# The next image's Walsh transform is moved beside its norms, its convolution is let in one pair at a time, and GpSimd gets no transform

## The chip, the cores and the metric

The kernel runs on one core of a Trainium2 chip. The metric is device time in microseconds (us). Before the change it is 11163.44 us, the median of three runs (11158.33 to 11166.24); the profiled execution has a span of 11170.1 us. Times inside the program are given as us from the start of that span. PE is TensorE, DVE VectorE, ACT ScalarE, POOL GpSimd, and SP issues most of the transfers. All numbers are 32-bit floats.

## The reference, cut to what matters

Four layers follow one another. The first two hold the Mamba scans and take the span up to about 9080 us; the change doesn't touch them. The last stage of the kernel holds the layers 2 and 3, for four images of 192 channels and 64 x 64 points:

```python
# layer 2: depthwise 3x3 convolution; its weights come from a small network on the pooled image.
# MASK keeps the upper row and the left neighbour: four taps a channel
wt = wt.reshape(b * DIM, 1, K, K) * jnp.tile(MASK, (b, 1, 1, 1))
out = jax.lax.conv_general_dilated(x.reshape(1, b * c, h, w), wt, ...)
...
# layer 3
xn = layer_norm(x.transpose(0, 2, 3, 1), norm1_g, norm1_b).transpose(0, 3, 1, 2)
xw = get_window(xn)                  # 4x4 windows: 16 positions, each of 192 channels
wf = sedenion_full_weight(w_sed)     # wf[i, k] = sum_j SED_TABLE[i, j, k] * w_sed[j]
xw = xw @ wf
x1 = reverse_window(xw, c)
y = x1.transpose(0, 2, 3, 1)
y = jax.nn.gelu(y, approximate=False)
y = y @ proj_w + proj_b
x = x + y.transpose(0, 3, 1, 2)
hbr = layer_norm(x.transpose(0, 2, 3, 1), norm2_g, norm2_b)
hbr = jax.nn.gelu(hbr @ fc1_w + fc1_b, approximate=False)
hbr = hbr @ fc2_w + fc2_b
x = x + hbr.transpose(0, 3, 1, 2)
```

In the sedenion product, output position k takes input i with weight i XOR k, with a sign. With signs put on inputs, weights and outputs, most of the 256 terms become a plain XOR convolution. A Walsh transform over the 16 positions turns that into 16 separate products. The terms whose sign does not fit are added directly from the normed input.

## The kernel before

The 16 positions are kept as 8 pairs g (the code's `NP`), each a tile of 128 partitions x 3 x 256. One image b goes through: convolution of 8 pairs (`prepare`), norm of each pair (`first_norm`), Walsh transform (`forward`), 16 products (`spectrum`), transform back (`inverse`), then for each pair k the direct terms (`product`), projection and second norm (`project`), and the two-layer network (`mlp`).

`Lanes` is a static scheduler. The main program emits matmuls and calls `tick()` between small groups of them; each tick lets each lane emit one more piece. So it fixes the order of the instructions on every engine. At run time each engine takes its own in that order and waits with semaphores.

```python
xh = const.tile([128, NP + 2, 3, NWIN], F32, name="xh")   # 10 slots for transformed pairs
at = list(range(NP))                                       # slot of each pair
spare = deque(range(NP, NP + 2))                           # two free slots

def normed(v, which, sq):                 # used by both norms
    mean = bank("mean"); each(full(mean), ones, v, [ALL, ALL])          # PE
    d = work.tile([128, 3, NWIN], F32, name=f"d{which}", bufs=1)
    nc.vector.tensor_tensor(d[:, 0::2, :], v[:, 0::2, :], mean[:, :, W], ALU.subtract)
    ...                                                                 # two more for the middle part
    nc.scalar.activation(sq, d, AF.Square)
    yield 3
    var = bank("var"); each(full(var), ones, sq, [ALL, ALL])            # PE
    nc.scalar.activation(rs, var[:, :, W], AF.Sqrt, bias=eps)
    nc.vector.reciprocal(rs, rs)
    nc.gpsimd.tensor_tensor(d[:, 0::2, :], d[:, 0::2, :], rs, ALU.mult) # and two more on GpSimd
    ...
    yield 6
    return d

def prepare(b):                           # convolution, lane 2
    for g in range(NP):
        i2, j = divmod(g, WIN)
        if j == 0:
            img = first if b == i2 == 0 else load(b, i2)   # 8 transfers, one buffer
        while g >= XW and (b, g - XW) not in read:
            yield 1
        v = work.tile([128, 3, NWIN], F32, name="xw", bufs=XW)
        for c in range(3):
            for tap in (3, 0, 1, 2):
                ...  # tap 3 on ACT (affine), taps 0 to 2 on DVE (scalar_tensor_tensor)
                yield 1
        nc.sync.dma_start(kept[b, g], v)
        lanes.add(3, first_norm(b, g, v))

def first_norm(b, g, v):                  # lane 3
    d = yield from normed(v, 1, sq)
    ...                                   # three affine on ACT: xn (image 0) or sq
    if b:
        nc.sync.dma_start(stored[b, g], t)    # put by in DRAM until the image's turn
    ready.add((b, g))

def butterfly(engine, s, d, a, b):
    engine.tensor_tensor(s, a, b, ALU.add)
    engine.tensor_tensor(d, a, b, ALU.subtract)

def both(v, to):                          # the transform's step inside a pair
    ...                                   # ACT: two copies into swapped
    butterfly(nc.vector, to[:, 0, :], to[:, 2, :], v[:, 0, :], v[:, 2, :])
    nc.vector.scalar_tensor_tensor(to[:, 1, :], v[:, 1, :], flip, swapped, ALU.mult, ALU.add)

def across():                             # the three steps across pairs: 12 butterflies
    n = 0
    for bit in (4, 2, 1):
        for a in range(NP):
            if a & bit:
                continue
            s, d = at[a], at[a | bit]
            to = spare.popleft()
            engine = nc.gpsimd if n % 3 == 1 else nc.vector
            butterfly(engine, xh[:, to], xh[:, d], xh[:, s], xh[:, d])
            at[a] = to; spare.append(s); n += 1
            yield 1

def forward(b):                           # lane 4
    for g in range(NP):
        both(xn[b, g], xh[:, at[g]]); yield 1
    yield from across()
    turned.add(b)

def inverse(b):                           # lane 4
    yield from across()
    for g in range(NP):
        ...  # both(xh[:, old], xh[:, to]) through a spare slot
        back.add((b, g)); yield 1

def product(b, k):
    for cols, made in zip((main, side), slots(k)):
        ps = psum_s.tile([128, 2, 2, NWIN], F32, name="sed_ps")   # two such tiles in all
        ...                               # PE: 92 records a pair in the profile; a tick between slots
        lanes.until(lambda: (b, k) in back)
        ...                               # DVE: six additions of ps and xh into y

lanes.add(4, walsh_weights())             # 24 GpSimd instructions, into xh as scratch
lanes.add(2, prepare(0))
for b in range(NB):
    lanes.until(lambda: (b, NP - 1) in ready and "weights" in turned)
    if b:
        fetch(b)                          # 8 loads of xn from DRAM
    lanes.add(4, forward(b))
    lanes.until(lambda: b in turned)
    if b + 1 < NB:
        lanes.add(2, prepare(b + 1))
    for g in range(NP):
        spectrum(g)
    lanes.add(4, inverse(b))
    for k in range(NP):
        ...
        lanes.add(0, project(b, k, product(b, k), x3))
lanes.drain()
```

Of the kernel before, what the change touches and what calls it, by code (L numbers as in the profile page):

```python
# [21 lines left out]
NB = 4  # L22
# [1057 lines left out]
def conv_and_windows(tc, x, sums, packs, aps, out):  # L1080
# [11 lines left out]
    with ExitStack() as ctx:  # L1092
# [100 lines left out]


        xh = const.tile([128, NP + 2, 3, NWIN], F32, name="xh")
        at = list(range(NP))
        spare = deque(range(NP, NP + 2))
        w_main = const.tile([128, 16, C], F32, name="w_main")
        w_side = const.tile([128, NP, C], F32, name="w_side")

# [36 lines left out]
            return d  # L1237

        xn, kept, stored, outs = {}, {}, {}, {}
        read, ready, projected, through, closed = set(), set(), set(), set(), set()  # L1240
        turned, back = set(), set()

        def prepare(b):

            for g in range(NP):
                i2, j = divmod(g, WIN)
                if j == 0:
                    img = first if b == i2 == 0 else load(b, i2)
                while g >= XW and (b, g - XW) not in read:
                    yield 1  # L1250
                v = work.tile([128, 3, NWIN], F32, name="xw", bufs=XW)
                for c in range(3):
                    for tap in (3, 0, 1, 2):
                        o = v[:, c, :].rearrange("p (r c) -> p r c", c=HW // WIN)
                        at = j + tap % 3
                        src = img[:, c, :, tap // 3, at : at + HW - 3 : WIN]
                        wk = wt[:, c, tap, b : b + 1]
                        if tap == 3:
                            affine(o, src, wk, w["bias"][:, c : c + 1])
                        else:  # L1260
                            nc.vector.scalar_tensor_tensor(o, src, wk, o, ALU.mult, ALU.add)  # L1261
                        yield 1
                kept[b, g] = dram.tile([128, 3, NWIN], F32, name="kept", bufs=2 * NP)
                nc.sync.dma_start(kept[b, g], v)
                lanes.add(3, first_norm(b, g, v))

        def first_norm(b, g, v):

            sq = work.tile([128, 3, NWIN], F32, name="sq", bufs=1)
            d = yield from normed(v, 1, sq)  # L1270
            read.add((b, g))
            if b == 0:
                t = xn[b, g] = work.tile([128, 3, NWIN], F32, name="xn", bufs=NP)
            else:
                t = sq
            n = norm1[x_sign[position(g, 0)], x_sign[position(g, 1)]]
            for c in range(3):
                affine(t[:, c, :], d[:, c, :], n[:, 0, c : c + 1], n[:, 1, c : c + 1])
            if b:
                stored[b, g] = dram.tile([128, 3, NWIN], F32, name="ahead", bufs=NP)  # L1280
                nc.sync.dma_start(stored[b, g], t)
            ready.add((b, g))

        def fetch(b):
            for g in range(NP):
# [3 lines left out]
        def butterfly(engine, s, d, a, b):  # L1289
            engine.tensor_tensor(s, a, b, ALU.add)  # L1290
            engine.tensor_tensor(d, a, b, ALU.subtract)  # L1291

        def walsh_weights():


            for j in range(16):
                if w_sign[j] > 0:
                    nc.scalar.activation(sed[:, :, j, :], sed[:, :, j, :], AF.Copy, scale=-1.0)

            def split(v, bit):  # L1300
                return v.rearrange("p (h e l) -> p e h l", e=2, l=bit * C)

            one, two = (xh[:, 4 * i : 4 * i + 4].rearrange("p a b c -> p (a b c)") for i in range(2))
# [12 lines left out]

        def both(v, to):

            swapped = work.tile([128, NWIN], F32, name="swapped", bufs=2)
            for k in range(2):  # L1320
                nc.scalar.copy(swapped[half[k], :], v[half[1 - k], 1, :])
            butterfly(nc.vector, to[:, 0, :], to[:, 2, :], v[:, 0, :], v[:, 2, :])
            nc.vector.scalar_tensor_tensor(  # L1323
                to[:, 1, :], v[:, 1, :], flip, swapped, ALU.mult, ALU.add
            )

        def across():

            n = 0
            for bit in (4, 2, 1):  # L1330
                for a in range(NP):
                    if a & bit:
                        continue
                    s, d = at[a], at[a | bit]
                    to = spare.popleft()
                    engine = nc.gpsimd if n % 3 == 1 else nc.vector
                    butterfly(engine, xh[:, to], xh[:, d], xh[:, s], xh[:, d])
                    at[a] = to
                    spare.append(s)
                    n += 1  # L1340
                    yield 1

        def forward(b):
            for g in range(NP):
                both(xn[b, g], xh[:, at[g]])
                yield 1
            yield from across()
            turned.add(b)

        def inverse(b):  # L1350
            yield from across()
            for g in range(NP):
                to, old = spare.popleft(), at[g]
                both(xh[:, old], xh[:, to])
                at[g] = to
                spare.append(old)
                back.add((b, g))
                yield 1
# [7 lines left out]

        main, side = slice(0, 128), slice(128, C)

        def spectrum(g):

            v = xh[:, at[g]]
            ps, ends, sides = parts()
            for outs, cols in ((ends, main), (sides, side)):
                for start in (True, False):
                    for k in range(2):
                        if start:
                            wt, x = w_main[:, position(g, k), cols], v[:, 2 * k, :]
                        else:
                            wt, x = w_side[half[k], g, cols], v[half[k], 1, :]
                        nc.tensor.matmul(outs[k], wt, x, start=start, stop=not start)  # L1380
# [3 lines left out]
            nc.scalar.activation(v[:, 0::2, :], ps[:, :, W], AF.Copy, scale=-1.0 / 32)  # L1384

        def slots(k):

# [13 lines left out]
        def product(b, k):  # L1401


            y = work.tile([128, 3, NWIN], F32, name="y", bufs=2)
            for cols, made in zip((main, side), slots(k)):
# [5 lines left out]
                left = Counter(group(t) for slot in made for t in slot)  # L1411
                begun = set()
                for slot in made:
# [18 lines left out]
                v = xh[:, at[k]]  # L1432
                if cols == side:
                    nc.vector.tensor_tensor(y[:, 1, :], ps[:, 1, 0, :], v[:, 1, :], ALU.add)
                    nc.vector.tensor_tensor(y[:, 1, :], ps[:, 0, 0, :], y[:, 1, :], ALU.add)
                else:
                    for h in (1, 0):
                        for s in range(2):
                            o = y[:, 2 * s, :]
                            nc.vector.tensor_tensor(o, ps[:, h, s, :], o if h == 0 else v[:, 2 * s, :], ALU.add)  # L1440
            return y

        def signed_gelu(k, y):
# [80 lines left out]
        lanes.add(4, walsh_weights())  # L1524
        lanes.add(2, prepare(0))
        for b in range(NB):
            lanes.until(lambda: (b, NP - 1) in ready and "weights" in turned)
            if b:
                fetch(b)
            lanes.add(4, forward(b))  # L1530
            lanes.until(lambda: b in turned)
            if b + 1 < NB:
                lanes.add(2, prepare(b + 1))
            for g in range(NP):
                spectrum(g)
# [161 lines left out]
```

## Time and profile before

| in the whole span of 11170.1 us | busy us | share |
|---|---|---|
| PE (matmuls) | 9265.0 | 83% |
| DVE | 9136.7 | 82% |
| ACT | 6545.5 | 59% |
| POOL | 7206.1 | 65% |

The last stage begins with the first load of an image at 9082.7 us. The table below gives its parts by what PE executes; the borders are those used for the windows of the profile.

| stretch, us | length | PE busy | DVE busy | what it is |
|---|---|---|---|---|
| 9753 to 10233 | 480.0 | 383.73 | 248.90 | image 1, from the end of image 0's last product |
| 10120 to 10194 | 74.0 | 72.61 | 20.35 | two pairs late in image 1 |
| 10760 to 10800 | 40.0 | 37.78 | 9.46 | image 3, the products of the spectrum |
| 10800 to 10840 | 40.0 | 24.31 | 30.57 | image 3, the transform back |

How to read it: a share of busy time over the whole span says little here, since four fifths of it belong to the scans. A stage has to be read from windows, from who waits for whom in it, and from the instructions in order of time. In the window view each engine's busy time is followed by its number of instructions, and the last three columns are the TensorE clock that was granted (1.00 is full), the share of the DMA engines and GB/s. A matmul instruction of this program appears as two records.

### The profile page before, as it was taken

How to read it: one execution, taken by the hardware profiler on the slowest of the kernel's cores; microseconds unless marked ns; L12 is line 12 of the kernel's file. 1: busy time of each engine (PE TensorE's matmuls, PEld its weight loads, DVE VectorE, ACT ScalarE, POOL GpSimd, SP SyncE). 2: the span in 40 equal slices, each digit the busy share in tenths (PEclk: the TensorE clock that was granted, in tenths of full speed). 3: DMA queues.
4: the chain of work that ended last, by engine and by line, in shares of the span. 5: the costliest groups of instructions: out<-in, count | busy, mean ns of one | idle time of the engine just before them, and what ended most of it. 6: DMA issues, size and time to landing. Idle time of an engine off the chain costs nothing. (4 is left out here: it accounts for less than half of the span.)

```text
span 11170.1 us, 97554 instructions
## 1 busy us (share of the span) xinstructions
PE 9265.0 (83%) x31324; PEld 3673.1 (33%) x31324; DVE 9136.7 (82%) x7831; ACT 6545.5 (59%) x9766; POOL 7206.1 (65%) x2768
## 2 busy tenths in 40 slices
PE   7888888888878888887689999999999854978788
PEld 2222222222223222222233333333333322545455
DVE  7999999999999999999688888788878837364542
ACT  5666666666666666666466666666666613333333
POOL 6888888888888888888466566566656622021110
PEclk7777777777777777777789889898889866989899
DMA  5666666666666666666455454454445422122110
GB/s 149 178 178 179 182 172 181 180 173 183 175 182 178 175 179 176 182 179 171 123 138 141 128 140 133 128 137 135 133 129 137 125 47 54 36 51 46 37 30 19
DMA packets 954743, 1506.97 MB, mean 135 GB/s; under 512 B 229834, under 2 KB 262638, under 8 KB 953846
## 3 DMA queue, kind: packets, MB, share of 16 engines
q1 hardware_dynamic: 953006, 1493.27, 49.8%
q10 hardware_dynamic: 1224, 7.47, 0.2%
q8 instruction: 247, 4.05, 0.2%
q14 instruction: 266, 2.18, 0.1%
HBM read 1289.65 MB, written 210.76 MB: 134 GB/s over the span
## 5 line engine op out<-in xcount | busy, mean ns | idle before, releaser
L570 DVE TENSOR_TENSOR_SCAN h<-dA,m_state,h 128x512 f32<-128x512 f32 x3840 | 4670.9, 1266 | 487.7 <-ACT dA L564 425.3
L586 POOL TENSOR_TENSOR h<-h,C 128x2048 f32<-128x2048 f32 x960 | 4342.0, 4527 | 625.8 <-ACT m_state L583 520.4
L564 ACT ACTIVATE dA<-dtE,m_A 128x512 f32<-128x512 f32 x4608 | 3106.1, 687 | 1308.8 <-DVE h L570 1194.2
L557 DVE TENSOR_TENSOR h<-dtxE,B 128x2048 f32<-128x2048 f32 x960 | 2170.6, 2261 | 116.8 <-DMA dtxE<-r_dtx 104.1
L595 PE MATMUL y<-h,gather 128*32 128x512 f32 x7680 | 1283.0, 747 | 402.3 <-POOL h L586 329.1
L448 PE MATMUL ps_in<-xT,m_in_w 96*128 96x512 f32 x1536 | 948.6, 765 | 250.4 <-ACT raw L451 132.0
L1233 POOL TENSOR_TENSOR d<-d,rs 128x512 f32<-128x512 f32 x64 | 86.5, 1351 | 1419.1 <-DVE rs L1232 1419.1
L466 PE MATMUL ps_conv<-raw,m_conv 128*128 128x512 f32 x2112 | 992.7, 619 | 1.7 <-ACT xc L471 1.7
L570 DVE TENSOR_TENSOR_SCAN h_apart<-dA,m_state,h_apart 128x512 f32<-128x512 f32 x768 | 922.5, 1260 | 39.6 <-ACT dA L564 39.6
L586 POOL TENSOR_TENSOR h_apart<-h_apart,C 128x2048 f32<-128x2048 f32 x192 | 869.4, 4528 | 45.6 <-ACT m_state L583 43.4
L557 POOL TENSOR_TENSOR h_apart<-dtxE,Bs 128x2048 f32<-128x2048 f32 x192 | 869.5, 4529 | 6.0 <-ACT Bs L546 6.0
L448 PEld LDWEIGHTS ps_in<-xT,m_in_w 96*128 96x128 f32 x1536 | 352.2, 242 | 821.9 <-issue 422.5
L585 POOL COPY m_state<-h 128x4 f32<-128x4 f32 x384 | 71.9, 187 | 850.0 <-DVE h L570 815.3
L466 PEld LDWEIGHTS ps_conv<-raw,m_conv 128*128 128x128 f32 x2112 | 418.2, 202 | 602.2 <-issue 568.1
L992 PE MATMUL ps_dw<-strip,dw 96*96 96x512 f32 x1152 | 574.4, 646 | 1.3 <-ACT x L1001 0.9
L595 PEld LDWEIGHTS y<-h,gather 128*32 128x32 f32 x7680 | 164.2, 117 | 1213.8 <-POOL h L586 570.2
L502 POOL TENSOR_TENSOR raw<-dt,xc 128x1536 f32<-128x1536 f32 x96 | 329.8, 3436 | 293.8 <-ACT dt L501 293.8
L482 PE MATMUL ps_x<-xc,m_pack 128*44 128x512 f32 x576 | 351.0, 758 | 198.0 <-ACT xc L478 194.7
L1421 PE MATMUL sed_ps<-xn,sed 64*128 64x256 f32 (+3 forms) x2944 | 496.1, 413 | 15.7 <-DVE y L1440 15.7
L564 ACT ACT_TABLE_LOAD x345 | 442.6, 1283 | 14.8 <-DMA dtE<-r_dt 8.5
L448 PE MATMUL ps_in<-xn,m_in_w 96*128 96x512 f32 x768 | 398.7, 666 | 47.4 <-ACT z L451 31.1
L375 PE MATMUL ps_o<-hid,t 128*96 128x512 f32 x768 | 390.8, 649 | 37.2 <-ACT hid L368 16.9
(192 smaller groups left out, 12506.9 us busy)
## 6 DMA issues: line engine op xcount, KB each, us to landing
dtE<-r_dt SPq DMA_DIRECT2D x2304, 256.0 KB, 5.0
dtxE<-r_dtx SPq DMA_DIRECT2D x2304, 256.0 KB, 4.2
r_dt<-dt SPq DMA_DIRECT2D x96, 768.0 KB, 4.0
r_dtx<-raw SPq DMA_DIRECT2D x96, 768.0 KB, 6.0
x<-x SPq DMA_DIRECT2D x64, 384.0 KB, 3.6
img<-x SPq DMA_DIRECT2D x28, 512.0 KB, 7.1
xt<-in_x SPq DMA_DIRECT2D x32, 384.0 KB, 5.6
x<-o SPq DMA_DIRECT2D x32, 384.0 KB, 4.9
```

Of the source, the lines that this page charges most:

```text
L375: nc.tensor.matmul(ps, self.w2[:, m, bass.ts(k, CP)], h[:, m, :], start=(m == 0), stop=(m == NH - 1),)
L448: nc.tensor.matmul(ps, self.in_w[:, k, bass.ts(e, 128)], xn[:, k, :], start=(k == 0), stop=(k == 1))
L466: nc.tensor.matmul(ps, self.conv[:, d, j, :], raw[:, d, j : j + T], start=(j == 0), stop=(j == K - 1))
L482: nc.tensor.matmul(ps, self.x_w[:, d, :], xc[:, d, :], start=(d == 0), stop=(d == ND - 1))
L502: nc.gpsimd.tensor_tensor(dtx, dt, xc, ALU.mult)
L557: engine.tensor_tensor(h, u["rows", k // 2, 1], u[B, k % 2].unsqueeze(1).broadcast_to([128, 4, T]), ALU.mult)
L564: self.nc.scalar.activation(dA, u["rows", k // 2, 0][:, j, :], AF.Exp, scale=self.A[:, k, j : j + 1])
L570: self.nc.vector.tensor_tensor_scan(h[:, j, :], u.pop(("dA", k, j)), h[:, j, :], self.state[:, k, j : j + 1], ALU.mult, ALU.add,)
L586: nc.gpsimd.tensor_tensor(h, h, u["C", k % 2].unsqueeze(1).broadcast_to([128, 4, T]), ALU.mult)
L595: self.nc.tensor.matmul(u["ys"][32 * j : 32 * j + 32, :], self.ex.gather[:, i // 2, :], h[:, j, :], start=(i == 0), stop=(i == 3 and not s ...
L992: nc.tensor.matmul(ps, dw[:, k, j, :], s[:, k, dy : dy + rows, dx : dx + HW], start=(j == 0), stop=(j == 8),)
L1421: nc.tensor.matmul(out, sed[p, int(h is not None), i ^ position(k, s), cols], xn[b, g][p, c, :], start=group(t) not in begun, stop=left[gr ...
```

## The change

The transform of an image no longer waits for all its norms and for its turn. Each norm of the next image goes on to `both` into a slot of `xh`, and then takes all butterflies for which the pairs are there (`settle`). Slots come free one at a time, as `product(k)` of the image in work has read its own. The transform back is also done step by step as the spectrum's products come in. The next image's convolution of pair g is let in only when the image in work has reached pair g - 1, and its pieces are spaced by two ticks. All butterflies are on DVE. The scratch of `walsh_weights` moves from `xh` to two work tiles whose names are used later. In image 0, where nothing else runs, the norms alternate between two lanes with a `d` each.

```diff
-        at = list(range(NP))
-        spare = deque(range(NP, NP + 2))
+        at = [[None] * NP for _ in range(NB)]
+        spare = deque(range(NP + 2))
...
 def prepare(b):
-                while g >= XW and (b, g - XW) not in read:
+                while g >= XW and (b, g - XW) not in read or b and g > reached[b - 1] + 1:
                     yield 1
...
-                        yield 1
+                        yield 2 if b else 1
...
-                lanes.add(3, first_norm(b, g, v))
+                lanes.add(1 if b == 0 and g % 2 else 3, first_norm(b, g, v))
 def first_norm(b, g, v):
-            sq = work.tile([128, 3, NWIN], F32, name="sq", bufs=1)
-            d = yield from normed(v, 1, sq)
+            i = 2 if b == 0 and g % 2 else 1
+            sq = work.tile([128, 3, NWIN], F32, name="sq", tag=("sq", "xn2")[i - 1], bufs=i)
+            if b:
+                yield 3
+            d = yield from normed(v, i, sq)
...
-            ready.add((b, g))
+            while settled[b] < g or len(spare) < 2:
+                yield 1
+            at[b][g] = spare.popleft()
+            both(t, xh[:, at[b][g]])
+            yield 1
+            yield from settle(at[b], g)
+            settled[b] += 1
...
-        def across():
-            ... engine = nc.gpsimd if n % 3 == 1 else nc.vector
+        def settle(v, g):
+            for bit in (1, 2, 4):
+                if (g + 1) % (2 * bit):
+                    return
+                for a in range(g + 1 - 2 * bit, g + 1 - bit):
+                    s, d, to = v[a], v[a + bit], spare.popleft()
+                    nc.vector.tensor_tensor(xh[:, to], xh[:, s], xh[:, d], ALU.add)
+                    nc.vector.tensor_tensor(xh[:, d], xh[:, s], xh[:, d], ALU.subtract)
+                    v[a] = to
+                    spare.append(s)
                     yield 1
-        def forward(b): ...
         def inverse(b):
-            yield from across()
+            for g in range(NP):
+                while (b, g) not in made:
+                    yield 1
+                yield from settle(at[b], g)
...
 def product(b, k):
+            spare.append(at[b][k])
             return y
...
         for b in range(NB):
-            lanes.until(lambda: (b, NP - 1) in ready and "weights" in turned)
+            lanes.until(lambda: settled[b] == NP and "weights" in turned)
             if b:
                 fetch(b)
-            lanes.add(4, forward(b))
-            lanes.until(lambda: b in turned)
             if b + 1 < NB:
                 lanes.add(2, prepare(b + 1))
+            lanes.add(4, inverse(b))
             for g in range(NP):
-                spectrum(g)
-            lanes.add(4, inverse(b))
+                spectrum(b, g)
             for k in range(NP):
                 n = b * NP + k
+                reached[b] = k
```

More of the change, by code (lines that the diff above doesn't have):

```diff
@@ L1239, in conv_and_windows @@
         xn, kept, stored, outs = {}, {}, {}, {}
-        read, ready, projected, through, closed = set(), set(), set(), set(), set()
-        turned, back = set(), set()
+        read, projected, through, closed = set(), set(), set(), set()
+        turned, made, back = set(), set(), set()
+        settled = [0] * NB
+        reached = [-1] * NB
         def prepare(b):
@@ L1287, in fetch @@
                 nc.sync.dma_start(t, stored.pop((b, g)))
-        def butterfly(engine, s, d, a, b):
-            engine.tensor_tensor(s, a, b, ALU.add)
-            engine.tensor_tensor(d, a, b, ALU.subtract)
         def walsh_weights():
@@ L1301, in split @@
                 return v.rearrange("p (h e l) -> p e h l", e=2, l=bit * C)
-            one, two = (xh[:, 4 * i : 4 * i + 4].rearrange("p a b c -> p (a b c)") for i in range(2))
+            one, two = (work.tile([128, 16 * C], F32, name=n, tag=n, bufs=1) for n in ("o", "hid"))
             for i in range(2):
@@ L1321, in both @@
                 nc.scalar.copy(swapped[half[k], :], v[half[1 - k], 1, :])
-            butterfly(nc.vector, to[:, 0, :], to[:, 2, :], v[:, 0, :], v[:, 2, :])
+            for i, op in ((0, ALU.add), (2, ALU.subtract)):
+                nc.vector.tensor_tensor(to[:, i, :], v[:, 0, :], v[:, 2, :], op)
             nc.vector.scalar_tensor_tensor(
@@ L1325, in both, with inverse @@
             )
-        def across():
[L1329 to L1338, printed above, removed]
+        def settle(v, g):
[7 more added lines that the diff above has]
+                    v[a] = to
                     spare.append(s)
-                    n += 1
                     yield 1
-        def forward(b):
+        def inverse(b):
             for g in range(NP):
-                both(xn[b, g], xh[:, at[g]])
-                yield 1
-            yield from across()
-            turned.add(b)
-        def inverse(b):
-            yield from across()
+                while (b, g) not in made:
+                    yield 1
+                yield from settle(at[b], g)
             for g in range(NP):
-                to, old = spare.popleft(), at[g]
+                to, old = spare.popleft(), at[b][g]
                 both(xh[:, old], xh[:, to])
-                at[g] = to
+                at[b][g] = to
                 spare.append(old)
@@ L1367, in conv_and_windows, with spectrum @@
         main, side = slice(0, 128), slice(128, C)
-        def spectrum(g):
-            v = xh[:, at[g]]
+        def spectrum(b, g):
+            v = xh[:, at[b][g]]
             ps, ends, sides = parts()
@@ L1384, in spectrum @@
             nc.scalar.activation(v[:, 0::2, :], ps[:, :, W], AF.Copy, scale=-1.0 / 32)
+            made.add((b, g))
         def slots(k):
@@ L1404, in product @@
             y = work.tile([128, 3, NWIN], F32, name="y", bufs=2)
-            for cols, made in zip((main, side), slots(k)):
+            for cols, terms in zip((main, side), slots(k)):
                 ps = psum_s.tile([128, 2, 2, NWIN], F32, name="sed_ps")
@@ L1409, in group @@
                     return t[0], t[0] if t[2] is None else t[2]
-                left = Counter(group(t) for slot in made for t in slot)
+                left = Counter(group(t) for slot in terms for t in slot)
                 begun = set()
-                for slot in made:
+                for slot in terms:
                     for t in slot:
@@ L1431, in product @@
                 lanes.until(lambda: (b, k) in back)
-                v = xh[:, at[k]]
+                v = xh[:, at[b][k]]
                 if cols == side:
```

## The prediction

> **What bounds the kernel now.** I read the slices of the page first: up to slice 32 the scans keep DVE full, and the change does not touch them. In the last eight slices the fullest engine is PE, and neither it nor anything else is full all the time. So I cut this stage into windows of 40 us (columns: length; PE, PE weight loads, DVE, ACT, POOL busy with their counts; clock; DMA share; GB/s). Four windows of image 1:
>
> ```profile
> 9840.00:9880.00 40.00, 26.34 (x114) 15.49 (x112) 35.96 (x35) 14.63 (x26) 12.54 (x7) 0.79 0.24 71
> 9880.00:9920.00 40.00, 14.55 (x59) 8.08 (x58) 28.13 (x42) 11.26 (x23) 12.74 (x9) 0.62 0.61 98
> 9920.00:9960.00 40.00, 29.77 (x143) 16.54 (x142) 30.72 (x42) 16.58 (x24) 6.30 (x7) 0.83 0.14 50
> ...
> 10160.00:10200.00 40.00, 39.94 (x228) 25.25 (x225) 12.43 (x21) 15.21 (x16) 2.68 (x3) 1.00 0.03 11
> ```
>
> The stage has two regimes. At an image's start DVE is nearly full, PE starves and its clock sinks; later PE is full at clock 1.00 and DVE is two thirds idle. Every image repeats this. The waits of PE for image 1 (9760 to 10240) name the cause:
>
> ```profile
> PE mean L1208 <- DVE xw L1261: 46.4, 4, 21.1
> PE ps_h L1208 <- ACT xn L1216: 10.9, 5, 4.2
> PE var L1208 <- ACT sq L1226: 8.7, 4, 4.3
> PE ps_o L1506 <- ACT hid L1493: 7.8, 3, 4.6
> PE ps_proj L1208 <- ACT y L1449: 6.6, 3, 3.4
> PE sed_ps L1380 <- DVE xh L1290: 6.4, 1, 6.4
> ```
>
> PE takes its instructions in order. The first norm's mean of the *next* image stands in its queue and waits for the convolution on DVE, and the current image's matmuls wait behind it. DVE is late because the forward transform, the transform back and the whole next convolution fall into the same 150 us. In the order of time on DVE I saw that a butterfly half takes 0.96 us, but 2.44 while GpSimd does one:
>
> ```profile
> 9790.47 0.96 DVE L1291 TENSOR_TENSOR xh<-xh 128x768 f32<-128x768 f32 x1
> 9791.35 0.95 DVE L1290 TENSOR_TENSOR xh<-xh 128x768 f32<-128x768 f32 x1
> 9792.34 2.44 DVE L1291 TENSOR_TENSOR xh<-xh 128x768 f32<-128x768 f32 x1
> 9794.81 2.44 DVE L1290 TENSOR_TENSOR xh<-xh 128x768 f32<-128x768 f32 x1
> ...
> 9801.63 2.44 DVE L1290 TENSOR_TENSOR xh<-xh 128x768 f32<-128x768 f32 x1
> ```
>
> The chain of waits late in the image gives the period of one pair when PE alone sets it:
>
> ```profile
> 10158.54 2.88 PE ps_proj L1208 x16
> ...
> 10195.10 2.88 PE ps_proj L1208 x16
> ```
>
> That is 36.56 us for product, projection, second norm and network, without a first norm.
>
> **What the Trainium skill says.** "SBUF — State Buffer", section "SBUF: two separate sides": DVE and GpSimd share a port pair as an exclusive lock; against a GpSimd operation that reads SBUF, a DVE operation with two SBUF inputs is blocked. The trace agrees: 0.96 becomes 2.44 us. "GPSIMD Engine Reference", section "3.1 Elementwise": elementwise work is about half as fast there as on DVE. Here a half butterfly is 2.40 us on POOL, so moving it to DVE costs 0.96 us and saves DVE a blocked 1.48. "TensorE: Matmul & The Clock Gate", section "What's actually happening": an idle PE falls to half clock. The windows show it, 0.62 in the starved one and 1.00 in the full one; the sixteen records of one pair's spectrum take 5.2 us cold, from 9323.59 to 9328.82, and 2.9 warm, from 10791.80 to 10794.66.
>
> **The change part by part.**
>
> *Entry (9082 to 9323).* The transform's start moves, the sum barely. Before, d of pairs 1 to 7 run from 9169.7 to 9281.0 in six periods, mostly of 17.7 us: DVE 12.3 (nine taps, two or three subtractions, a reciprocal of 3.35), two waits of 2.65 and 2.9. The transform follows, and spectrum starts at 9323.6. The order of instructions after shows reciprocal, four taps, then `both`, which needs POOL (3.3) and ACT (0.6 + 1.1 + 0.8) after the reciprocal: 5.8 less 3.3 of taps is a new wait of 2.5, and `both` itself is 1.3. Period 17.7 + 3.8 = 21.5, six of them 129, plus five settled pairs at 1.9 (10), plus one image wait (5): pair 7's d at 9314. Then 5 to its reciprocal, 3.35, 6, `both` 1.3, and four of its seven butterflies (7.6) before the first product can start: 9337. I take 9330, so nothing is gained here. Two lanes don't help while the order on DVE is serial.
>
> *Floor of an image.* Spectrum 8 x 2.9 = 23 (2.86 above), eight pairs at 36.6 = 293, eight first norms at 2 x 1.6 = 26: 342 us for image 1 or 2, 316 for image 3, which prepares nothing. Now images 1 and 2 take 480 each.
>
> *DVE, per pair.* Nine taps 6.1, two norms' subtractions 3.0, two reciprocals 6.7, `both` 1.3, 1.5 butterflies 2.9, six additions to y 2.4, four of the projection 1.8, three of o 2.0: 26, and some 4 of lock by POOL's multiplications: 30 of a pair's 40. So DVE is not the bound on average, and POOL's 32 butterflies add 64 x 0.96 = 61 us of DVE over the stage while removing about as much blocking.
>
> *What remains as waits.* (a) Inside a pair. The order of instructions shows in many pairs two reciprocals one after the other and both norms' multiplications on POOL. The second norm's chain gets up to 3.35 + 3.3 us longer; late in image 1 it just fits (var ends at 10170.3, the first ps_h on it is at 10179.6, and root, table, reciprocal, multiplication and affine are 0.7 + 1.3 + 3.35 + 3.3 + 1.8 = 10.4). PE's own 3.2 of first norm pays part of it. I take 4 us a pair, 32 an image. (b) The inverse. In image 3 before, with no next image, PE waited once for 15.7 us (DVE y at 10828.39). After, DVE must do, between an image's last y and the next image's first: 12 butterflies 23, eight `both` 10.4, taps 10, two subtractions and reciprocals 10, o and projection 6: some 65 with locks. PE has in the same stretch projection 3, spectrum 23, network outputs 16, two norms 7, ps_h 10, product 14: 73. Nearly balanced; I take 15 us at images 1 to 3 and 20 at image 0, where no network runs beside it. (c) The next image's load. The first pair's affine on ACT stands right at the spectrum in the order, and its load stands behind eight xn loads in SP's queue. Before, those loads held the DMA engines from 9750 to 9764 (0.95 busy), and the second half of an image needed 7.8 us from issue to its first affine (9901.5 to 9909.3). ACT blocks till some 15 us after the last product, PE has work for 5: 10 us at images 1 and 2. The other half image is issued a pair ahead of its use and is hidden.
>
> *Sum.* Image 0, to its last product: spectrum 34, cold and with a hole as before from 9323.6, + 8 x 39.8 less the work still owed at that point (projection, norm, two network outputs, one ps_h: 33) = 319; plus 20 + 32 = 371: 9330 to 9701 (before 9753). Images 1 and 2: 342 + 32 + 15 + 10 = 399 each: 10499. Image 3: 316 + 15 + 8 = 339: 10838. Tail, last product to end, as before 11170 - 11106 = 64: 10902. Gain 268 of the traced 11170. From 11163 that is 10895.
>
> **The rivals.** *DVE stays the bound.* DVE is at 36 of 40 where the streams meet now, and the change adds butterflies. If DVE ran at 0.9 throughout, an image needs (26 x 8 + 33) / 0.9 + 40 of locks = 308, still under 399. So it can only bound locally; were every pair to take 47 us instead of 44, 72 us would go: 10965. The window 9920 to 9960 speaks for it: norms of both kinds there, and PE only at 29.77. But there the convolution runs two pairs per product, and PE is still filling. *The lost time was PE's cold clock and comes back fully.* If in-order waits vanish, pairs take 40 and images start without a hole: 10902 - 96 - 65 = 10740 traced. What speaks against it is that 10.4 us chain. *The loads collide.* If the image's three thirds land over 30 us behind xn, ACT could block three times: 20 us more at two images, 40 in all. *The slots starve.* A norm waits in its lane until a slot is free; it would hold back the next spectrum. Slots come free a pair ahead of need, and the order of matmuls after shows the spectrum following directly on the last product, with no gap in emission, so I give it little.
>
> **Range and chances.** The term with most weight is (a): 2 to 7 us a pair over 24 pairs, -48 to +72. The starts of the images add ±40, the entry ±20. Together about 65 as a deviation: 10800 to 10990 for 8 in 10, around 10890. The 2% line is 10940, 50 us above: 0.76 to be faster by more, 0.22 within, 0.02 slower. For slower nearly every stall would have to come back and grow.
>
> **What would show it.** In the changed kernel the 40 us windows from 9400 on should hold PE at 34 to 38 and DVE at 25 to 32, without one below 25 but at image starts; POOL should have no xh butterflies and half butterflies on DVE should be 0.96 throughout, bar those beside a norm. The wait of mean for xw should fall from 46 us to under 10 an image. The spectrum of image 0 should still start within 20 us of 9323; if it starts 40 earlier, my serial reading of the entry is wrong. Intervals between projections should be 42 to 46 in images 0 to 2 and 37 in image 3. At image starts ACT should show one idle stretch before xw, ended by img, of about 10 us. I am wrong if pairs take over 47 us, or if the first y of an image comes more than 95 us after the last y of the one before.

## The result, and the profile after

The changed kernel takes 10982.54 us (median of 4 runs, 10981.56 to 10984.23); the kernel before took 11164.84 in the same session. The ratio is 0.984, with a 95% interval from 0.982 to 0.986: 1.6% faster. The prediction was 10890, with a range up to 10990. So the time lies in the range, 92 us above its middle, and the likeliest of the three outcomes (faster by over 2%) did not come.

The first spectrum starts at 9323.5, as before, and the gain is all behind it. Each row below goes from the end of one image's last product to the end of the next one's (image 0: from the first spectrum), with the waits of PE added up. The wait ahead of the first spectrum (36.9 us before, 16.2 after) is not in image 0's.

| stretch | before: us, waits | after: us, waits | predicted us |
|---|---|---|---|
| image 0 | 428.1, 79.8 | 385.8, 52.2 | 371 |
| image 1 | 475.6, 93.8 | 426.7, 59.4 | 399 |
| image 2 | 480.1, 93.2 | 426.7, 59.7 | 399 |
| image 3 | 397.4, 54.4 | 356.1, 20.8 | 339 |
| tail | 65 | 62.7 | 64 |

The windows of 40 us in image 1 after, with the columns as before (length; PE, weight loads, DVE, ACT and POOL busy; clock; DMA share; GB/s):

```profile
9800.00:9840.00 40.00, 18.99 (x94) 9.66 (x93) 26.65 (x54) 12.85 (x25) 2.66 (x3) 0.70 0.19 51
9840.00:9880.00 40.00, 31.01 (x163) 17.59 (x162) 14.05 (x21) 17.71 (x21) 3.21 (x3) 0.96 0.06 20
9880.00:9920.00 40.00, 33.86 (x158) 20.58 (x160) 20.70 (x28) 12.04 (x19) 6.41 (x7) 0.83 0.16 41
...
10080.00:10120.00 40.00, 40.00 (x232) 25.55 (x228) 22.06 (x32) 17.98 (x23) 5.98 (x7) 1.00 0.09 30
```

The two regimes are gone but for one window: DVE, which held 36 of 40 at the start of image 1, stays between 14 and 28, and PE starves only where the transform back lies (18.99 of 40). The waits of PE in image 1 after (9709 to 10136; total, times, longest):

```profile
PE ps_proj L1208 <- ACT y L1453: 22.3, 3, 10.5
PE mean L1208 <- DVE xw L1263: 15.2, 2, 14.7
PE ps_h L1208 <- ACT xn L1216: 10.4, 5, 3.4
PE ps_o L1510 <- ACT rs L1231: 2.9, 2, 1.8
PE ps_o L1510 <- ACT hid L1497: 2.7, 2, 1.4
```

The wait of mean for the convolution, 46.4 before, is now one stretch of 14.7 and a rest; a wait of the projection for ACT has come up. The longest of each, on PE (start, length, what; in brackets the idle time before it and what ended it):

```profile
9727.03 4.80 PE L1208 MATMUL ps_proj<-y,t_bw 128*128 128x256 f32 x16 [10.45 <-ACT y L1453]
9815.10 2.38 PE L1208 MATMUL mean<-xw,ones 128*128 128x256 f32 x6 [14.69 <-DVE xw L1263]
```

What both of these are is seen in the order of time. First ACT, after the last product of image 0:

```profile
9711.02 0.69 ACT L1216 ACTIVATE hid<-ps_h,t_bv 128x512 f32<-128x512 f32 x1 [2.03 <-PE ps_h L1208]
9723.84 0.84 ACT L1216 ACTIVATE xw<-img,t_bv,wt 128x256 f32<-128x256 f32 x1 [12.13 <-DMA img<-x]
9724.58 0.67 ACT L1216 ACTIVATE hid<-ps_h,t_bv 128x512 f32<-128x512 f32 x1
9725.27 1.28 ACT L1453 ACT_TABLE_LOAD   x1
```

ACT stands at the affine of image 2's first half for 12.13 us, because that half has not been loaded, and the gelu of y, which the projection needs, stands behind it in the order. SP's queue shows why the load is late:

```profile
9706.57 4.99 SPq L1299 DMA_DIRECT2D xn<-ahead  x8
9711.66 0.40 SPq L1119 DMA_DIRECT2D img<-x  x1
```

The load is issued behind the eight xn loads, 12 us before ACT can go on. Second, DVE at the end of the transform back:

```profile
9711.73 0.42 DVE L1437 TENSOR_TENSOR y<-sed_ps,xh 128x256 f32<-128x256 f32 x1
...
9801.49 0.76 DVE L1331 TENSOR_TENSOR xh<-xh 128x256 f32<-128x256 f32 x2
...
9811.76 1.38 DVE L1263 SCALAR_TENSOR_TENSOR xw<-img,wt,xw 128x256 f32<-128x256 f32 x2
9813.06 0.75 DVE L1443 TENSOR_TENSOR y<-sed_ps,xh 128x256 f32<-128x256 f32 x2
```

About 101 us lie between the last y of image 0 and the first y of image 1. From 9801.5 to 9811.8 DVE does `both` (L1331, L1332) of all eight pairs one after the other, with some taps of the convolution between them, before the first y, though that y needs only pair 0.

### The profile page after: what moved, and what is told of

Same layout as the page of the kernel before. It is cut to its first block, busy times and chain, and to the rows that moved or that the text cites. A ratio compares the mean times of both kernels' runs of the same rounds, so it can differ in the third digit from the quotient of the medians.

```text
span 10981.5 us, 97463 instructions
## 1 busy us (share of the span) xinstructions
PE 9199.4 (84%) x31324; PEld 3647.6 (33%) x31324; DVE 9103.9 (83%) x7895; ACT 6559.9 (60%) x9778; POOL 7062.7 (64%) x2704
```

## The experiments

Each kernel ran in three rounds beside the kernel before; ratios are to that kernel, with 95% intervals.

### The parts of the change

**Letting in alone (e1).** The kernel before, with the next image's convolution let in pair by pair and in larger steps:

```diff
-while g >= XW and (b, g - XW) not in read:
+while g >= XW and (b, g - XW) not in read or b and g > reached[b - 1] + 1:
-                        yield 1
+                        yield 2 if b else 1
+                reached[b] = k
```

> The kernel before with nothing but the gate: the next image's pair g is convolved only when the image in work has reached pair g-1, with two ticks between pieces; transforms stay where they were, with their third on GpSimd. If the burst of the next convolution at an image's start is half of what was lost, the wait of the mean for xw falls from 46 us to about 10 an image and three images gain 30 each: 11075 us. If the place of the forward transform is nearly everything, the time stays at 11140 or above.

11092.41, ratio 0.993 (0.992 to 0.995), 76 us less: near the theory's 11075 in time, but only partly in the wait. Image 0 is 36 us shorter, images 1 and 2 18 and 23, where 30 each were expected. PE's wait of mean for xw in image 1:

```profile
PE mean L1208 <- DVE xw L1262: 32.7, 2, 25.8
```

It was 46.4 in four waits, and is 32.7 in two. What is left is mainly one wait of 25.8. It lies at the transform back, which this kernel still does in one block.

**All butterflies on DVE alone (e9).** The kernel before, without the letting in:

```diff
-engine = nc.gpsimd if n % 3 == 1 else nc.vector
+engine = nc.vector
```

> The kernel before with nothing but its butterflies all on DVE. e3 lost 34 us by putting a third on GpSimd in the changed kernel. In the kernel before, the forward transform stands alone on the path at each image's start: its 12 butterflies take from about 9775 to 9805 at image 1, 30 us with DVE blocked, and would take 23. If both transforms gain 5 to 7 us at each of four images: 11110 to 11130 us. Rival: DVE is so full at that place that the four butterflies taken over cost what the blocking cost: 11160 or more.

11131.34, ratio 0.997 (0.995 to 0.998): 38 us less.

**Both (e10).**

> The kernel before with the gate of e1 and all butterflies on DVE: everything of the change but the transform's new place and the inverse by steps. If the parts add up, e1's 76 us and e9's gain, some 11050 us; then 70 us are left for the transform's place. If the gate has already taken the load from DVE that made GpSimd's blocking costly, 11075 or more.

11061.58, ratio 0.991 (0.989 to 0.992): 108 us less, and 76 + 38 is 114. The two parts are nearly independent. From here to the changed kernel there are 79 us more. They belong to what these kernels don't have: above all the next image's transform beside its norms, in slots given back, and the transform back by steps. Those were not taken apart further.

**A third back on GpSimd (e3).** The changed kernel with every third butterfly there:

```diff
+engine = nc.gpsimd if flies[0] % 3 == 1 else nc.vector
+flies[0] += 1
-nc.vector.tensor_tensor(xh[:, to], xh[:, s], xh[:, d], ALU.add)
+engine.tensor_tensor(xh[:, to], xh[:, s], xh[:, d], ALU.add)
```

> The changed kernel with every third butterfly on GpSimd again. A butterfly takes 4.8 us there and 1.9 on DVE, and it blocks DVE meanwhile. If DVE is no bound outside the starts of images, only the chain of the transform back (seven butterflies, two or three of them on GpSimd) gets longer, by 6 to 9 us at each of four starts: 11005 to 11020 us. If taking GpSimd out is the main gain, 11060 or more. If it is worth nothing, 10982 +- 8.

11016.28, 34 us slower than the changed kernel. The half butterflies left on DVE in one image (shortest, median, longest ns), by operation and form:

```profile
L1347 DVE TENSOR_TENSOR xh<-xh x17: 957/958/2453, 9724.1 to 10157.8; 128x768 f32<-128x768 f32 x17
```

Most of them are undisturbed at 0.96, since they are now spread out; a few meet GpSimd and take up to 2.45. In this image DVE waits longer for the results of GpSimd's butterflies than it loses by such meetings (under 4 us); its idle time before operations on xh contains

```profile
POOL xh L1347: 13.1, 4
POOL xh L1346: 1.7, 1
```

So a longer chain through GpSimd, as the expectation had it, is the likelier cause; the two were not separated. Images 1 and 2 lose 7 us each, and image 0 loses 15.

**No letting in (e2).** The changed kernel without the condition on `reached`:

```diff
-while g >= XW and (b, g - XW) not in read or b and g > reached[b - 1] + 1:
+while g >= XW and (b, g - XW) not in read:
```

> The changed kernel without the gate, all else kept. If the gate matters beside the slots, three pairs are convolved at once at each image's start, the mean waits for xw there some 10 to 15 us longer than the 14.7 of the changed kernel, and three images lose that: about 11020 us. Rival: the slots that come free one at a time already hold the norms back, and with three xw buffers the convolution too, so the gate adds nothing: 10982 +- 10.

10984.46, the time of the changed kernel (images again 426.7). The rival was right. The reading is that a norm has to wait in its lane for a slot, so that the slots pace the next image and the condition adds nothing. In the kernel before, where there are no such slots, it was worth 76 us together with the larger steps, which e2 keeps.

**One lane for the first norms (e8).** The changed kernel with one lane and one d in image 0 instead of two:

```diff
-lanes.add(1 if b == 0 and g % 2 else 3, first_norm(b, g, v))
+lanes.add(3, first_norm(b, g, v))
-i = 2 if b == 0 and g % 2 else 1
+i = 1
```

> The changed kernel with all norms of image 0 in one lane and one d and sq, as before the change. If the order on DVE makes the entry serial in any case, as the prediction reads it, the spectrum starts within 3 us of 9323.5 and the time is 10982 +- 6. Rival: the second d lets norms overlap and has paid for the transform beside them; then the entry gets 15 us or more longer: 10997 or more.

10981.74: no difference. The spectrum starts at 9318.0, 5.5 earlier than with two lanes (3 were expected at most), and images 0 and 1 take it back. The second lane is worth nothing.

### The waits, and the 80 us that did not come

My first theory for the missing time was the cold clock: in image 1 after, PE stands at half clock for 54.6 us, and I had reckoned every operation at full clock.

**The waits filled (e4).** Superfluous matmuls, whose results are overwritten, stand where PE waits longest, so that it stays warm:

```diff
# first norm of the second pair, in images 1 to 3
+for _ in range(30):
+    nc.tensor.matmul(mean[:, 0, W], ones[:, 0, :], v[:, 0, :], start=True, stop=True)
# ahead of the projection
+for _ in range({0: 14, 1: 12, NP - 1: 24}.get(k, 0) if b < NB - 1 else 0):
+    nc.tensor.matmul(ps[:, 0, W], w["proj_w"][:, 0, main], x3[:, 0, :], start=True, stop=True)
```

> The changed kernel with superfluous matmuls whose result is overwritten, put where PE waits in images 0 to 2: 30 before the mean of the next image's second pair (wait 14.7 us), 14, 12 and 24 before the projections of pairs 0, 1 and 7 (waits 6.3, 5.5, 10.5). They add work only where PE stands still. If the missing 25 us an image are PE at half clock after each wait, the half-clock time falls from 55 us an image to under 25 and the three images gain some 13 to 15 each: 10940 us. Rival: other engines set the pace there and a faster PE only waits more, or my floor for an image is too low: 10982 +- 8, though the clock is higher.

10979.06, 3.5 us less than the changed kernel. Image 1 in one window, first after, then with the waits filled:

```profile
9709.30:10136.00 426.70, 367.26 (x2017) 224.60 (x2017) 239.33 (x337) 181.02 (x254) 50.27 (x51) 0.94 0.23 52
```

```profile
9708.10:10127.40 419.30, 394.29 (x2177) 251.42 (x2177) 239.26 (x337) 181.03 (x254) 50.23 (x51) 0.98 0.24 53
```

The time at half clock fell from 54.6 to 17.1 us, the waits from 59 to 25. The records of the matmuls put in, 60 before mean and 100 before the projections, took 13.2 and 22.3 us, 35.5 in all and all at full clock. PE's other records took 359.3 us, 8.0 less than the 367.3 of after, and the image is 7.4 shorter, about half of the 13 to 15 expected. (Image 3 lost 9, as the 24 at the end of image 2 stand where no wait is: no image is loaded there. That, and a gain of only 0.3 in image 0, is why so little is left in the total.)

Why it is not more is seen when the clock's records are laid over PE's. Of the 54.6 us at half clock PE works in only 31.5; in the others it waits and loses nothing. With the waits filled, 14.2 us of its own work are left at half clock: 17.3 less, and half of that is 8.6. The last column takes half of the half-clock work off the busy time (all of image 1, us):

| kernel | PE busy | of it at half clock | busy less half of that |
|---|---|---|---|
| before | 381.6 | 57.9 | 352.6 |
| e1 | 375.3 | 45.3 | 352.6 |
| after | 367.3 | 31.5 | 351.5 |
| e4, without the matmuls put in | 359.3 | 14.2 | 352.2 |
| e7 | 367.6 | 32.1 | 351.6 |
| e12 | 363.2 | 23.9 | 351.3 |
| e11 (120 records fewer) | 351.1 | 28.4 | 336.9 |

Whatever the order, PE's work in image 1 needs 351 to 353 us at full clock, and each us of it that the record shows at half clock would take half a us at full clock. So the first theory was right for a part: the cold clock is 15.7 of the 25 us that are missing in image 1. The window also showed where to look for the rest: I had allowed 342 for this work, and even at full clock it is 351.5.

**The load ahead (e5), `both` one by one (e6), and the two together (e7).** Two remedies for the two waits:

```diff
# e5
-img = first if b == i2 == 0 else load(b, i2)
+img = ahead.pop(b) if i2 == 0 else load(b, i2)
+if b + 1 < NB:                     # at the end of prepare
+    ahead[b + 1] = load(b + 1, 0)
# e6, in inverse, before both(g)
+while g and (b, g - 1) not in drawn:
+    yield 1
```

> The changed kernel, with the first half image of the next image but one loaded as soon as the last pair of the one before has left the buffer, ahead of the xn loads in SP's queue, not at the start of the spectrum. If ACT's block on img at the start of images 1 and 2 is what makes PE wait 10.5 us for the projection there, both waits go: 10982 - 21 = 10961 us. Rival: the projection stands in a chain that fills the hole with another wait, or the early load delays the last loads of x: 10975 or more.

> The changed kernel, with the last step of the transform back (both) of pair g let in only after the first sums of pair g - 1, not all eight in a row. Seven of them are 8.6 us of DVE ahead of the first sums of an image. If DVE's chain ahead of the mean of the next image's second pair is what PE waits 14.7 us for, that wait falls to about 6 in images 0 to 2: 10982 - 25 = 10957 us. Rival: the taps of the convolution set it, then it moves little: 10975 or more.

> e5 and e6 together. The two waits are at different places (one before the spectrum's end, one after it), so the gains should add up: 10937 us if both theories hold.

10961.65, 10959.69 and 10938.17: 21, 23 and 44 us less than the changed kernel, all within 3 us of what was expected. The 10.5 us wait of the projection is gone in e5 and the 14.7 of mean is 7.5 in e6 (what sets the rest was not looked into). Image 1 with both:

```profile
9703.50:10113.50 410.00, 367.68 (x2017) 225.43 (x2018) 239.27 (x338) 181.00 (x254) 50.26 (x51) 0.95 0.24 54
```

The image is 16.7 us shorter, the waits are 17.1 shorter (42.3), and PE's busy time has not moved: 367.68. Waits taken away come back as time, whole, and the work of 367 stays.

**Five terms (e11).** My second theory: the pair from which I had taken the floor has a small product. The groups of the kernel before in that interval, 10158.54 to 10195.10 (busy us, mean ns), and those of the changed kernel in image 1, show it:

```profile
L1421 PE MATMUL sed_ps<-xn,sed 128*128 128x256 f32 x20 | 5.4, 395 | 0.0
L1421 PE MATMUL sed_ps<-xn,sed 128*64 128x256 f32 x20 | 3.2, 392 | 0.0
```

```profile
L1424 PE MATMUL sed_ps<-xn,sed 128*128 128x256 f32 x184 | 52.8, 407 | 1.7 <-DVE y L1443 1.7
L1424 PE MATMUL sed_ps<-xn,sed 128*64 128x256 f32 x184 | 28.0, 414 | 0.0
```

The interval holds 20 records of each of four forms, 80 in all; eight pairs have 184 of each, which is 92 a pair. The direct terms of the eight pairs are 14, 12, 12, 8, 12, 12, 10 and 12, with eight records each, and the interval was that of the seventh. e11 leaves 15 of these 92 terms out, so that no position has more than five (its output is then not the convolution's):

```diff
-n = [rest[position(k, s)] for s in range(2)]
+n = [list(rest[position(k, s)]) for s in range(2)]   # and, while longer than 5, one is taken out
```

> The changed kernel with at most five direct terms for each of the 16 output positions: 77 terms an image instead of 92, so 15 x 8 = 120 of the 736 matmul records of an image's products are left out (the output is then not the convolution's). In the changed kernel those 736 records take 124.1 us of image 1, 0.169 each, and PE's busy time in the image is 0.92 of the sum over its operations. My theory now: PE's own work sets an image, and my floor was short because the pair I took it from has the second smallest product (80 records; the mean is 92). Then the records left out come back whole: 120 x 0.169 x 0.92 = 18.7 us of PE's busy time in an image (367.3 to about 348.6), the waits stay within 5 us of 60, and the four images together give 60 to 80 us: 10905 to 10922. Rival: a pair is set by the chain of the second norm on DVE and ACT or by the lanes' order, and PE's work lies beside it; then the waits grow by what PE's work shrinks, and the time stays at 10950 or above.

10861.69, 121 us less than the changed kernel, where 60 to 78 were expected. PE's busy time in image 1 fell to 351.15, by 16.1 where 18.7 was expected: this part held. With the half clock taken off it is 14.6, or 0.12 us a record. But the waits also fell, from 59 to 37, which neither theory had. A product gives the other lanes a step after each slot of terms. With fewer slots it gave fewer steps, and so the order of all that follows moved. The run does not separate the two.

**Fewer steps, all terms (e12).** The changed kernel with every term, but with only as many steps in a product as e11 has, spread evenly:

```diff
-for cols, terms in zip((main, side), slots(k)):
+for cols, terms, few in zip((main, side), slots(k), slots(k, 5)):   # slots with at most 5 terms
-    lanes.tick()
+    if (at_slot + 1) * len(few) // len(terms) > at_slot * len(few) // len(terms):
+        lanes.tick()
```

> The changed kernel with all 92 terms, but with as many steps of the lanes in each product as the kernel with at most five terms has, spread evenly over the product's slots. That kernel gained 121 us where the left-out records account for about 16 us of PE's busy time in an image (367.3 to 351.2); the rest, by the waits (60 to 37 in image 1), came with fewer steps: the last pair's network then reaches into the next spectrum and covers the wait for the image's load and most of the transform back. My theory: the two add up. Keeping the terms puts 16 us back into each of four images, so 10862 + 64 = 10926 (10912 to 10940), PE's busy time of image 1 back at 365 to 370 and the waits at 35 to 45. Rival: the waits fell because the products were short and left the engines' chains time elsewhere, not because of the order; then the waits come back to about 60 and the time to 10970 or more.

10879.11, ratio 0.974 (0.973 to 0.976): 103 us less than the changed kernel by the order alone, and 2.6% less than the kernel before. It is the fastest of those that compute the whole. My expectation, 10926, was too high: the waits are 29 in image 1 (35 to 45 expected). Image 1 in one window:

```profile
9671.40:10063.50 392.10, 363.19 (x2021) 225.13 (x2017) 235.97 (x337) 185.58 (x258) 49.33 (x51) 0.97 0.25 57
```

PE's busy time is 363.19 with all terms against 351.15 with 77, under nearly the same order: 12 us for the terms left out, or 14.4 with the half clock taken off. ACT at the same place as above:

```profile
9673.17 0.69 ACT L1216 ACTIVATE hid<-ps_h,t_bv 128x512 f32<-128x512 f32 x1 [3.26 <-PE ps_h L1208]
9673.88 1.28 ACT L1458 ACT_TABLE_LOAD   x1
9675.17 0.72 ACT L1458 ACTIVATE y<-y 128x256 f32<-128x256 f32 x2
```

The gelu of y now stands ahead of the affine on the unloaded image, so the projection does not wait. How the order keeps PE from waiting at the transform back was not taken apart. More of the last pair's network now lies between the products of the spectrum: 73 records of ps_h where the changed kernel has 56, in a stretch of about the same length (62.5 and 63.9 us). The waits of the projection and of mean, which e5 and e6 shortened (22.3 and 15.2 in all after the change), are not among those of this image any more. Whether e5 and e6 would add anything here was not tried.

## Why the prediction was right or wrong

**The step that failed is the floor of an image**, "eight pairs at 36.6 = 293" and with it 342 us: the mechanism of waits was right, and this term was too small. PE is busy for 367 us in images 1 and 2, 25 more than the term, for 335 in image 3 (316 predicted), and for 334 in image 0, where the sum had 371 with 52 of waits, so 319. That is 84 us in the four images. The waits came out 3 us above their terms in all, the start 6.5 and the tail 1 below, and this makes up the 80 us by which the traced end, 10981.5, lies above my 10902.

The floor lacks two things. The larger is the clock: 36.6 for a pair and 2.9 for a pair's spectrum are both from stretches at full clock, and PE does 31.5 us of image 1 at half clock, which is 15.7 us more. The prediction had the halving before it, 5.2 us cold against 2.9 warm, and gave it no term. The other is the pair from which the floor was taken: at full clock too the work is 351.5, and 9.5 are missing. The 36.6 was measured rightly, and it returns in image 3 of the changed kernel, where the projections are

```profile
10735.35 2.92 PE L1208 MATMUL ps_proj<-y,t_bw 128*128 128x256 f32 x16 [1.02 <-ACT y L1453]
10764.85 2.93 PE L1208 MATMUL ps_proj<-y,t_bw 128*128 128x256 f32 x16
10807.25 2.92 PE L1208 MATMUL ps_proj<-y,t_bw 128*128 128x256 f32 x16
10849.91 2.92 PE L1208 MATMUL ps_proj<-y,t_bw 128*128 128x256 f32 x16
10886.47 2.92 PE L1208 MATMUL ps_proj<-y,t_bw 128*128 128x256 f32 x16
```

29.5, 42.4, 42.7 and again 36.6 apart, with 172, 235, 243 and 210 records of PE between them. The 36.6 is the seventh pair's number and not a pair's. Its product has 12 records fewer than the mean; at the 0.12 us a record that e11 shows, eight pairs lack 11.5 us by it. So the other terms of the floor were some 2 us too large.

That the time stayed in the range is luck in part. The range was made from the waits, the starts and the entry, which came out right, and had nothing for the floor.

**The waits were right, one by one.** (a) 32 us in the pairs: the projections' wait without the load's part (11.8), ps_h 10.4, ps_o 5.7 and some small ones of 6 in all come to 34. (b) 15 for the inverse: 14.7. (c) 10 for the load: 10.5, with ACT blocked for 12.13 at the place named. 57 were predicted and 59 measured. That the waits are real and lie on the path was shown by e5, e6 and e7.

**The entry came out near its number**: 9323.5 for 9330, where the parts had added up to 9337. The new wait at `both` is 0.76 instead of 2.5, and pair 7's d stands at 9301.7 instead of 9314.

**DVE is not the bound**: right, and with more room than I said (14 to 28 of 40 where 25 to 32 were named). That GpSimd's butterflies cost DVE what they spare it was read from 0.96 against 2.44 us and from the Trainium skill's "SBUF — State Buffer", section "SBUF: two separate sides". In the kernel before the trace agrees, and they cost even more: with all on DVE (e9) its busy time is 9112.6 us instead of 9136.7. In the changed kernel, where the butterflies are spread out, it is not so: with a third of them back on GpSimd (e3) DVE's busy time is 9081.0 instead of 9103.9, 23 less. What the sum had no term for is that the kernel is 34 to 38 us slower with them (e3, e9), in e3 mostly by PE's waits (image 0: 52 to 63 us).

**The rivals.** DVE as the bound had the nearest number, 10965, but not the cause: pairs do take 45.9 us in the mean of image 0 (37 to 51; 42 to 46 were named), and DVE is busy for only 239 us of an image of 427. The one that time at cold clock comes back fully (10740) is wrong only in "fully". Of the 49 us that image 1 gained, 14 are PE's busy time, 381.6 to 367.3, and the work at half clock fell from 57.9 to 31.5 us; the 15.7 that it still costs did not come back. "TensorE: Matmul & The Clock Gate", section "What's actually happening", says an idle PE falls to half clock. The trace agrees: the projection's sixteen records take 4.80 us after the wait of 10.45 and 2.92 where PE has not waited. The rival of loads that collide did not happen: one load of an image blocks, once. Slots seem to pace the next image (e2), but they hold back no spectrum: image 1's begins 1.6 us after image 0's last product.

**What I named as signs.** An image's first y more than 95 us after the last y was to prove me wrong, and it was 101. I took it for a sign of long waits, but of the 101 only 25 are the two large waits; the rest is PE's work in the stretch, which I had put at 73. The wait of mean under 10 us contradicted my own term (b), which had 15.

## What to carry to other kernels

Before one interval becomes the floor of a stage, count the instructions in it against those of the whole stage, or take the busy time of the bounding engine over a whole unit: here 80 against 92 records said a part of it before any run. And look at the clock that this interval had and the one that the stage has: 1.00 and 0.94 here. Engines that take instructions in order wait for whatever stands next, so how many steps a long operation yields to the others is a parameter like the number of buffers: fewer steps in the product gave 103 us, more than half of what the whole change had brought. Two throttles on the same flow, the slots and the letting in, did not add here.

## What the runs showed of the hardware

Half clock in the record costs half, but only where PE works. In the twelve kernels with every term and nothing put in, PE's busy time in image 1 runs from 363 us (e12) to 384 (e9), and less half of what it worked at half clock it is 351 to 353 in each. Of the 54.6 us at half clock after the change, 23 lie in waits and cost nothing. So time at half clock is to be laid over PE's work before it is counted as lost: filling the waits took 37.5 us of it away and shortened PE's own work by 8.0 (e4).

A half butterfly on DVE that meets one on GpSimd takes about 2.44 us instead of 0.96. The one on GpSimd gets longer too: 1.80 us where DVE does nothing beside it, and often 2.4 to 2.6 where DVE works (e3).
